# A state-space layer, linear attention and an FFN in one kernel: attention tokens transposed and stored by channel where their norm is made, and the FFN chains behind the main loop regrouped

## The chip, the cores and the metric

The kernel runs on one core of a Trainium2 chip. The metric is the device time of one execution in microseconds, as the median of three runs. The core has five engines with an instruction queue each, worked through in order: TensorE (PE in the profile; its weight loads are PEld), VectorE (DVE), ScalarE (ACT), GpSimd (POOL), and SyncE (SP), from which nearly all DMA transfers are issued. They meet only through semaphores.

## What is computed

The input x has 8 images of 96 channels and 64 x 64 pixels, so 4096 tokens of 96 channels each. Two layers follow each other:

```
x = x + mamba(group_norm(x))          # in_proj, conv of 4, silu, selective scan over 4096 tokens
                                      # with 192 channels x 16 states, gate, out_proj, LayerNorm
t = tokens(x)
t = t + attn(ln(t))                   # 6 heads, no softmax: y = q (k^T v) * 16**-0.5, then Wff
t = t + ffn(ln(t))                    # 96 -> 384 -> 96, operands rounded to fp8 e5m2, sums to fp16
x = from_tokens(t)
```

Since the attention has no softmax, all of it is one 96 x 96 matrix per image: from the Gram matrix of the normalised tokens (97 x 97 with a column of ones for the biases) come a few small products (W in the code), and then each token is multiplied by the result.

## The kernel before

**Tiling.** Images are taken in 4 pairs (p), tokens in 8 chunks of 512 (c), which makes 32 chunks (p, c). Partitions of the scan hold 32 channels x 4 states; a chunk is 24 units (u), each a scan over 2 x 512 elements for one block of 64 inner channels, 4 states and one image of the pair.

**The main loop** runs under manual scheduling: instructions go into each engine's queue in the order of the Python code. `unit()` writes one unit: the copy of the last state (L619), the matmul that spreads C over partitions (L571), the sums over states of an earlier unit (L595), the products dbu of three units ahead on GpSimd (L561), two scans on VectorE (L639), between them two exponentials on ScalarE for the next unit (L581, two PSUM buffers `da`), and the product with C (L663).

**Chains.** All other work is cut into generators, and the table `STEPS` says in which units each makes its next step, ahead of the scan or (after the bar) behind it:

- P prepares the chunk two ahead: norm, conv, projections, delta (L431 on). Its conv results leave PSUM on ScalarE (xm, L468), its delta by L511.
- E finishes the last chunk: out_proj (L691), LayerNorm, the residual in x1 (L741, L746), a second norm into `t1e` (tokens on partitions, 96 channels and a column of ones), the Gram matrix (L759, added up by L768), and the stores of x1 (L750) and `t1e` (L780) to DRAM.
- W turns the Gram matrix of a pair into the matrix of the attention (L793 to L816).
- F, one for each image of a chunk, nine chunks later (`LAG`), as the Gram matrix needs all chunks of a pair: it loads `t1e` as `tp` (L826) and x1 as x2 (L827), transposes `tp` by four matmuls with the identity (L831), copies the result to SBUF (`tT`, L834), multiplies by the attention's matrix (L838), adds (L844), norms (L398 to L411), transposes (L854, L857), and runs the FFN: three matmuls (L864) with copies (L871), ReLU (L877 or L881) and rounding to fp8 (L884), three matmuls back (L903), bias (L910 or L912), a transpose of x2 (L915), the sum and the store (L918, L919).

F0 is the F of image 1 of the pair and starts in unit 20, F1 that of image 0 and starts in unit 9. In the main loop E, F, W and the norms of the next pair (G) share two PSUM banks, mE and mF; F uses mE up to L838 and mF behind it.

**Behind the main loop** (from line 1012 on) the scheduler of the framework orders each engine's instructions, in the main by the order of the code. `run_out` steps its generators in turn; with `lag` a new one joins every `lag` turns. Four calls follow each other: the rest of the running chains with the last E; the two F of the last chunk of pair 2 (`tail_f(NP - 2)`); the two W of pair 3; and the 16 F of pair 3 with four PSUM banks and a lag of four. In these F, `tp` and x2 have four buffers; o2, qT, h8 and y16 have one each and h16 two.

Of the kernel before, what the change touches and what calls it, by code (L numbers as in the profile page):

```python
# [8 lines left out]
F32 = mybir.dt.float32  # L9
F32R = mybir.dt.float32r  # L10
F16 = mybir.dt.float16
F8 = mybir.dt.float8e5
# [3 lines left out]
C = 96  # L16
# [4 lines left out]
T = 512  # L21
NK = T // 128
# [6 lines left out]
AHEAD = 3  # L29
# [5 lines left out]


STEPS = {
    0: "F0 F1",
    1: "F0 F1 P",
    2: "F1 | F0 G0",  # L40
    3: "E P F1 | F0 G6",
    4: "E F1 | G6",
# [6 lines left out]
    11: "F0 E",  # L49
    12: "F0 E | P",  # L50
    13: "P E F0",
    14: "P F0 | E F1",
    15: "F1 E F0 P | G5",
    16: "| E F1 F0 W1 P",
    17: "P | F1 W1",
    18: "P P | W1 F1",
# [1 line left out]
    20: "E F0 P | W1 F1",  # L58
    21: "F1 P | E",
    22: "F1 P E",  # L60
    23: "F1 P | E F0",
}


# [1 line left out]
def tile_mamba_linear_attention_ffn(  # L66
# [29 lines left out]
    nc = tc.nc  # L96
    B, _, L = x.shape
    NP = B // 2
# [19 lines left out]
        return t  # L118

    def psum(tag="mp"):  # L120
        return ps_all.tile([128, T], F32, tag=tag, name=tag, bufs=2 if tag == "cc" else 1)


    ident = const.tile([128, 128], F32, name="ident")
# [266 lines left out]
    def norm_stats(src, n, tag):  # L391

        mv = p2.tile([128, n, 2], F32, tag=f"mv{tag}", name="mv")
        rstd = p2.tile([128, n], F32, tag=f"rs{tag}", name="rs")
        nmr = p2.tile([128, n], F32, tag=f"nm{tag}", name="nm")
        st = p2.tile([128, n, 6], F32, tag=f"st{tag}", name="st")
        for i in range(n):
            nc.vector.bn_stats(st[:, i, :], src[:, i, :])  # L398
        for i in range(n):
            nc.vector.bn_aggr(mv[:, i, :], st[:, i, :])  # L400

        def ends():
            nc.gpsimd.tensor_scalar_mul(nmr, mv[:, :, 0], -1.0)  # L403
            rsqrt(rstd, mv[:, :, 1], 1e-5)
            nc.gpsimd.tensor_mul(nmr, nmr, rstd)

        later("norms", ends)
        return rstd, nmr
# [266 lines left out]
    gram = {}  # L675
    kept = {}

    def chain_e(p, c, s):
        zs = s["zs"]
        o = t1e[:, :, 0:C]  # L680

        def half(t, b):
            return t[:, b * NK : (b + 1) * NK, :]

        def project(part):

            ps = psum("mE")
            for k in range(2):
                tok = (2 * part + k) * 128
                for j in range(NJ):  # L690
                    nc.tensor.matmul(  # L691
                        ps[:, 2 * k * C : 2 * (k + 1) * C], lhsT=zs[:, j, tok : tok + 128],
                        rhs=woT[:, j].rearrange("p b c -> p (b c)"),
                        start=(j == 0), stop=(j == NJ - 1),
                    )
            return ps

        def projected(part, ps):
            nc.scalar.copy(  # L699
                o.rearrange("p (b k) c -> p k b c", b=2)[:, 2 * part : 2 * part + 2],  # L700
                ps[:, 0 : NK * C].rearrange("p (k b c) -> p k b c", k=2, b=2),
            )

        def tokens(b):
            ps = psum("mE")
            for k in range(NK):
                nc.tensor.matmul(
                    ps[:, k * C : (k + 1) * C], lhsT=xr[:, b, k * 128 : (k + 1) * 128], rhs=idb,
                    start=True, stop=True,
                )  # L710
            return ps[:, 0 : NK * C].rearrange("p (k c) -> p k c", c=C)

        def scale(dst, src, norm, part):
            for i in range(2 * part, 2 * part + 2):
                normalise(dst[:, i, :], src[:, i, :], norm, i)

        def gains(b):
            nc.gpsimd.tensor_mul(
                half(o, b), half(o, b), gamma.unsqueeze(1).to_broadcast([128, NK, C])
            )  # L720

        nc.sync.dma_start(
            xr[0:C], x[2 * p : 2 * p + 2, :, c * T : (c + 1) * T].rearrange("b c t -> c b t")
        )
        ps = project(0)
        yield
        projected(0, ps)
        ps = project(1)
        yield
        projected(1, ps)  # L730
        yield
        norm = norm_stats(o, 2 * NK, "o")
        yield
        for part in range(4):
            scale(o, o, norm, part)
            yield
        gains(0)
        ps = tokens(0)
        yield
        x1 = p1.tile([128, 2 * NK, C], F32, tag="x1", name="x1")  # L740
        nc.vector.tensor_add(half(x1, 0), ps, half(o, 0))  # L741
        yield
        gains(1)
        ps = tokens(1)
        yield
        nc.vector.tensor_add(half(x1, 1), ps, half(o, 1))  # L746
        norm = norm_stats(x1, 2 * NK, "x")
        yield
        x1d = dram.tile([128, 2 * NK, C], F32, tag="x1d", name="x1d", bufs=NCH + 4)
        nc.sync.dma_start(x1d, x1)  # L750
        scale(o, x1, norm, 0)
        scale(o, x1, norm, 1)
        yield

        def products(b):
            ps = psum("mE")
            for k in range(NK):
                t = t1e[:, b * NK + k, :]
                nc.tensor.matmul(  # L759
                    ps[0 : C + 1, 0 : C + 1], lhsT=t, rhs=t, start=(k == 0), stop=(k == NK - 1)  # L760
                )
            return ps[0 : C + 1, 0 : C + 1]

        def collect(b, ps):
            if c == 0:
                nc.vector.tensor_copy(gram[p][:, b, :], ps)
            else:
                nc.vector.tensor_add(gram[p][:, b, :], ps, gram[p][:, b, :])  # L768

        if c == 0:  # L770
            gram[p] = p2.tile([C + 1, 2, C + 1], F32, tag="gram", name="gram")
        scale(o, x1, norm, 2)
        ps = products(0)
        yield
        collect(0, ps)
        scale(o, x1, norm, 3)
        yield
        ps = products(1)
        t1d = dram.tile([128, 2 * NK, C + 1], F32, tag="t1d", name="t1d", bufs=NCH + 4)
        nc.sync.dma_start(t1d, t1e)  # L780
        kept[p, c] = (x1d, t1d)
        yield
        collect(1, ps)


    attn_w = {}
# [29 lines left out]
        nc.vector.tensor_add(w[C : C + 1, b, :], ps[C : C + 1, 0:C], bffr[C : C + 1, :])  # L816


    def chain_f(p, c, b, banks, of_t1=None, of_x2=None):
        bank = banks[0]  # L820
        x1d, t1d = kept[p, c]
        blk = slice(b * NK, (b + 1) * NK)
        bufs = 4 if of_t1 else 1
        x2 = p2.tile([128, NK, C], F32, tag=of_x2 or f"x2{b}", name="x2", bufs=bufs)
        tp = p2.tile([128, NK, C + 1], F32, tag=of_t1 or "tp", name="tp", bufs=bufs)
        nc.sync.dma_start(tp, t1d[:, blk, :])  # L826
        nc.sync.dma_start(x2, x1d[:, blk, :])  # L827
        yield
        ps = psum(bank)
        for k in range(NK):  # L830
            nc.tensor.transpose(ps[0 : C + 1, k * 128 : (k + 1) * 128], tp[:, k, :], ident)  # L831
        yield
        tT = p2.tile([C + 1, T], F32, tag="rows", name="tT")
        nc.scalar.copy(tT, ps[0 : C + 1, :])  # L834
        yield
        ps = psum(bank)
        for k in range(NK):
# [7 lines left out]
        norm = norm_stats(x2, NK, f"f{b}")  # L845
        yield
        bank = banks[1]
        o2 = p1.tile([128, NK, C], F32, tag="o2", name="o2")
        for k in range(NK):
            normalise(o2[:, k, :], x2[:, k, :], norm, k)  # L850
        yield
# [1 line left out]
        for k in range(NK):  # L853
            nc.tensor.transpose(ps[0:C, k * 128 : (k + 1) * 128], o2[:, k, :], ident)  # L854
        yield
        qT = p1.tile([C, T], F8, tag="qT", name="qT")
        nc.scalar.activation(qT, ps[0:C, :], AF.Copy, saturate=False)  # L857
        yield
        h8 = []
# [7 lines left out]
            return ps  # L867

        def rounded(m, ps):
            h16.append(p2.tile([128, T], F16, tag="h16", name="h16"))  # L870
            nc.scalar.copy(h16[m], ps)  # L871

        def relu(m):
            if not m:
                h8.append(p1.tile([128, 3, T], F8, tag="h8", name="h8"))
            if of_t1:
                nc.vector.tensor_scalar(  # L877
                    h16[m], h16[m], b1q[:, m : m + 1], 0.0, ALU.add, ALU.max
                )
            else:  # L880
                nc.scalar.activation(h16[m], h16[m], AF.Relu, bias=b1q[:, m : m + 1])  # L881
            later(
                "others",
                lambda: nc.gpsimd.tensor_copy(h8[0][:, m, :], h16[m], saturate=False),  # L884
            )
# [18 lines left out]
                ps[0:C, :], lhsT=w2T[:, m, :], rhs=h8[0][:, m, :], start=(m == 0), stop=(m == 2)  # L904
            )
        yield
        y16 = p1.tile([C, T], F16, tag="y16", name="y16")
        nc.scalar.copy(y16, ps[0:C, :])
        if of_t1:
            nc.vector.tensor_scalar(y16, y16, b2q, None, ALU.add)  # L910
        else:
            nc.scalar.activation(y16, y16, AF.Identity, bias=b2q)  # L912
# [101 lines left out]
    gate(s, NJ - 1)  # L1014
    rest = [(p, c, b) for p in range(NP) for c in range(NCH) for b in range(2)]
    rest = rest[2 * (N - LAG) :]
    banks = ("mE", "mF", "cc", "y")

    def tail_f(p):
        return [  # L1020
            chain_f(*r, (banks[i % 4],) * 2, "dbu", "pr")
            for i, r in enumerate(r for r in rest if r[0] == p)
        ]

    run_out([*running.values(), chain_e(*chunks[N - 1], s)])
    run_out(tail_f(NP - 2), 4)
    run_out([chain_w(NP - 1, b, banks[b]) for b in range(2)])
    run_out(tail_f(NP - 1), 4)


# [51 lines left out]
```

## Time and profile before

| what | us |
|---|---|
| median of three runs (3532.91 to 3539.99) | 3535.59 |
| the profiled execution | 3550.77 |
| its span, first to last instruction | 3549.1 |
| VectorE busy | 3017.3 |
| TensorE busy, as modelled | 2708.4 |
| GpSimd busy | 2689.0 |
| ScalarE busy | 2277.4 |
| mean granted TensorE clock | 0.730 of full |

Times in the profile are counted from the start of the span. A row of the timeline has the start, the busy time, engine, line, operation, output and inputs, shapes, the number of instructions merged, and in brackets how long the engine was idle before and which instruction ended that. Matmul ends are modelled.

The chunks can be counted in the trace by their 48 scans. A chunk from the tenth on takes 98 to 109 us, one of the first nine, which have no F, 88 to 99 us. The last scan starts at 3366.2 us; what is behind it takes the remaining 183 us.

### The profile page before, as it was taken

What the parts mean: (1) busy time and instruction counts of PE and PEld (TensorE: products, weight loads), DVE (VectorE), ACT (ScalarE), POOL (GpSimd) and SP (SyncE); (2) the same over time, 40 slices, a digit from 0 to 9 for tenths busy, and PEclk for the clock granted to TensorE, in tenths of its full rate; (3) what the DMA queues carried; (4) which work ended last, traced back from release to release, by engine and by line L of the source; (5) the groups of instructions that cost most, each with busy time, mean ns of one, the idle gap of its engine ahead of it and who ended that gap; (6) DMA issues with size and microseconds to landing.
All of it is one profiled execution on the core that took longest, in us unless ns stands there. A gap on an engine that the chain in (4) does not pass through costs nothing.

```text
span 3549.1 us, 35756 instructions
## 1 busy us (share of the span) xinstructions
PE 2708.4 (76%) x9770; PEld 1011.7 (29%) x9770; DVE 3017.3 (85%) x4345; ACT 2277.4 (64%) x4347; POOL 2689.0 (76%) x1838
## 2 busy tenths in 40 slices
PE   5577777778787777877878877777788787887677
PEld 1122222222223222322223322222233232332244
DVE  2699999899998889888889888899888888988934
ACT  2456666566666666666666666666776766676556
POOL 1778888788878787778777778778877878777734
PEclk8667777677766787776787677778866777775667
DMA  2555555555554456554456554455544445545212
GB/s 80 127 128 139 134 141 142 143 131 133 136 149 107 104 139 154 138 129 108 112 139 154 131 138 105 117 134 150 149 124 121 99 121 144 152 119 139 72 59 61
DMA packets 252399, 444.05 MB, mean 125 GB/s; under 512 B 36965, under 2 KB 53542, under 8 KB 252198
## 3 DMA queue, kind: packets, MB, share of 16 engines
q1 hardware_dynamic: 248982, 441.70, 49.2%
q8 instruction: 77, 1.26, 0.2%
q14 instruction: 124, 1.02, 0.1%
q10 hardware_dynamic: 3216, 0.07, 0.1%
HBM read 349.24 MB, written 92.41 MB: 124 GB/s over the span
## 4 chain that ended last, share of the span: by engine, by line
DVE 39%; PE 25%; ACT 12%; issue 9%; POOL 7%; DMA 2%; SPq 1%; DVEq 0%; POOLq 0%; ACTq 0%
DVE hs L639 25%; PE mp L450 7%; DVE pr L663 7%; PE y L595 4%; POOL dbu L561 3%; DVE st L398 3%; ACT da L581 2%; PE cc L571 2%; PE mE L759 2%; PE mp L507 1%; PE mp L489 1%; PE mE L691 1%; POOL pr L670 1%; DVE mv L400 1%; DMA b<-bd 1%
## 5 line engine op out<-in xcount | busy, mean ns | idle before, releaser
L561 POOL TENSOR_TENSOR dbu<-du,b 128x1024 f32<-128x1024 f32 x768 | 1802.9, 2362 | 220.2 <-DVE hs L639 106.7
L639 DVE TENSOR_TENSOR_SCAN hs<-da,state,dbu 128x512 f32<-128x512 f32 x1290 | 1575.7, 1267 | 260.3 <-ACT da L581 252.2
L581 ACT ACTIVATE da<-dl,aneg 128x512 f32<-128x512 f32 x1474 | 999.1, 688 | 780.9 <-DVE hs L639 777.8
L663 DVE TENSOR_TENSOR pr<-hs,cc 128x1024 f32<-128x1024 f32 x640 | 777.6, 1215 | 36.8 <-DVE hs L639 0.5
L595 PE MATMUL y<-pr,ssum 128*32 128x512 f32 x3072 | 633.9, 883 | 4.9 <-DVE pr L663 4.9
L571 PE MATMUL cc<-cs,sel 64*128 64x512 f32 x640 | 397.2, 623 | 292.1 <-DVE pr L663 291.6
L450 PE MATMUL mp<-u,wk 96*64 96x512 f32 x1536 | 428.1, 683 | 90.3 <-ACT xm L468 86.9
L571 PEld LDWEIGHTS cc<-cs,sel 64*128 64x128 f32 x640 | 145.4, 229 | 932.3 <-DVE pr L663 423.0
L670 POOL TENSOR_TENSOR pr<-hs,c 128x1024 f32<-128x1024 f32 x128 | 301.7, 2357 | 122.6 <-DVE hs L639 96.4
L639 DVE TENSOR_TENSOR_SCAN hs<-da,dbu 128x512 f32<-128x512 f32 x184 | 213.5, 1207 | 110.9 <-ACT da L581 110.6
L884 POOL CAST h<-h 128x512 fp8e5<-128x512 f16 x192 | 117.5, 614 | 155.9 <-ACT h L881 109.9
L603 PE MATMUL y<-xm,dd 128*128 128x512 f32 x192 | 157.2, 913 | 99.5 <-DVE zs L609 99.3
L403 POOL TENSOR_SCALAR nm<-mv 128x8 f32<-128x8 f32 (+1 forms) x128 | 32.6, 255 | 238.8 <-DVE mv L400 222.0
L489 PE MATMUL mp<-xm,xpT 128*96 128x512 f32 x192 | 158.7, 994 | 48.7 <-ACT xm L483 48.0
L507 PE MATMUL mp<-dbl,dtT 12*128 12x512 f32 x192 | 168.0, 968 | 34.6 <-ACT cs L497 33.3
L864 PE MATMUL mF<-qT,w1T 96*128 96x512 fp8e5 x153 | 67.9, 444 | 157.1 <-ACT h L871 156.4
L450 PEld LDWEIGHTS mp<-u,wk 96*64 96x64 f32 x1536 | 105.0, 151 | 286.3 <-issue 162.9
L132 POOL TENSOR_TENSOR rs<-rs,mhalf 128x8 f32<-128x8 f32 (+1 forms) x128 | 173.5, 1355 | 10.7
L595 PEld LDWEIGHTS y<-pr,ssum 128*32 128x32 f32 x3072 | 75.2, 128 | 271.9 <-issue 228.1
L691 PE MATMUL mE<-woT,zs 128*128 128x192 f32 x768 | 142.9, 336 | 5.9 <-ACT t1e L699 4.3
L458 PE MATMUL mp<-u,wz 96*64 96x512 f32 x384 | 134.8, 788 | 14.6 <-ACT xm L476 11.7
L619 ACT COPY state<-hs 128x2 f32<-128x2 f32 x736 | 131.5, 179 | 0.2
(214 smaller groups left out, 3468.1 us busy)
## 6 DMA issues: line engine op xcount, KB each, us to landing
du<-lu SPq DMA_DIRECT2D x384, 256.0 KB, 5.2
dl<-ld SPq DMA_DIRECT2D x384, 256.0 KB, 7.2
b<-bd SPq DMA_DIRECT2D x512, 128.0 KB, 6.0
ld<-delta SPq DMA_DIRECT2D x96, 256.0 KB, 4.4
lu<-du SPq DMA_DIRECT2D x96, 256.0 KB, 4.9
c<-bd SPq DMA_DIRECT2D x128, 128.0 KB, 3.2
t1d<-t1e SPq DMA_DIRECT2D x32, 388.0 KB, 4.7
tp<-t1d SPq DMA_DIRECT2D x64, 194.0 KB, 5.9
```

Source lines behind the costliest of these rows:

```text
L132: nc.gpsimd.tensor_tensor(out_, out_, mhalf[0 : out_.shape[0], 0 : out_.shape[1]], op=ALU.pow)
L450: nc.tensor.matmul(ps[64 * b : 64 * b + 64, :], lhsT=wk[:, k, 64 * j : 64 * j + 64], rhs=u[:, b, k : k + T], start=(k == 0), stop=(k == 3),)
L489: nc.tensor.matmul(ps[0:C, :], lhsT=xpT[:, j, :], rhs=xm[:, j, :], start=(j == 0), stop=(j == NJ - 1),)
L507: nc.tensor.matmul(ps, lhsT=dtT[:, j, :], rhs=dbl[0 : 2 * RANK, :], start=True, stop=True)
L561: nc.gpsimd.tensor_mul(dbu, s["du", j][:, 2 * b : 2 * b + 2, :], s["b", g][:, b, :].unsqueeze(1).to_broadcast([128, 2, T]),)
L571: nc.tensor.matmul(cc, lhsT=sel[64:128, g, b], rhs=s["cs"][64:128, :], start=True, stop=True)
L581: nc.scalar.activation(da, s["dl", j][:, 2 * b + h, :], AF.Exp, scale=aneg[:, 2 * j + h, g : g + 1])
L595: nc.tensor.matmul(s["y"][q : q + 32, :], lhsT=ssum, rhs=pr[:, h, :], start=False, stop=(g == NG - 1),)
L639: nc.vector.tensor_tensor_scan(hs[:, h, :], s.pop(("da", u, h)), dbu[:, h, :], 0.0 if first else state["last"][:, u, h : h + 1], ALU.mult, ...
L663: nc.vector.tensor_mul(pr, hs, s.pop(("cc", u)).unsqueeze(1).to_broadcast([128, 2, T]))
L670: nc.gpsimd.tensor_mul(pr, s["hs", u], s["c", g][:, b, :].unsqueeze(1).to_broadcast([128, 2, T]))
L691: nc.tensor.matmul(ps[:, 2 * k * C : 2 * (k + 1) * C], lhsT=zs[:, j, tok : tok + 128], rhs=woT[:, j].rearrange("p b c -> p (b c)"), start= ...
```

## The change

1. **E transposes.** Behind the second Gram matrix, E transposes `t1e` image by image (four matmuls with the identity each), ScalarE copies the result to an SBUF tile `tT` [97, 512], and it is stored by channel. The store of `t1e` by token goes.
2. **F loads `tT` by channel** and multiplies at once. Its transposes and its ScalarE copy go, and two of its steps.
3. **STEPS** follow: E has two more steps, in units 0 and 1 of the next chunk; F0 loses the steps in units 23 and 0, F1 those in units 14 and 15.
4. **Behind the loop**: the running chains, the last E followed by the W of pair 3 (on banks `cc` and `mp`), and the two F of pair 2 (banks `y` and `da`) all run side by side; then the 16 F of pair 3 on six banks with a lag of three. Their tiles take buffers of the main loop: three for o2, two each for qT, h8 and y16, eight for x2, two h16 for even and two for odd chains.
5. The scratch `st` of the norms has one buffer in place of two.

```diff
@@ STEPS (lines that change)
-    0: "F0 F1",
-    1: "F0 F1 P",
+    0: "E F1",
+    1: "E F0 F1 P",
...
-    14: "P F0 | E F1",
-    15: "F1 E F0 P | G5",
+    14: "P F0 | E",
+    15: "E F0 P | G5",
...
-    23: "F1 P | E F0",
+    23: "F1 P | E",
@@ norm_stats
-        st = p2.tile([128, n, 6], F32, tag=f"st{tag}", name="st")
+        st = p1.tile([128, n, 6], F32, tag=f"st{tag}", name="st")
@@ chain_e(p, c, s, bank="mE"); every psum("mE") in it becomes psum(bank)
+        t1d = dram.tile([C + 1, 2, T], F32, tag="t1d", name="t1d", bufs=NCH + 4)
+
+        def transposed(b):
+            ps = psum(bank)
+            for k in range(NK):
+                nc.tensor.transpose(
+                    ps[0 : C + 1, k * 128 : (k + 1) * 128], t1e[:, b * NK + k, :], ident
+                )
+            return ps
+
+        def stored(b, ps):
+            tT = p2.tile([C + 1, T], F32, tag="rows", name="tT")
+            nc.scalar.copy(tT, ps[0 : C + 1, :])
+            nc.sync.dma_start(t1d[:, b, :], tT)
...
         ps = products(1)
-        t1d = dram.tile([128, 2 * NK, C + 1], F32, tag="t1d", name="t1d", bufs=NCH + 4)
-        nc.sync.dma_start(t1d, t1e)
+        yield
+        collect(1, ps)
+        ps = transposed(0)
+        yield
+        stored(0, ps)
+        ps = transposed(1)
+        yield
+        stored(1, ps)
         kept[p, c] = (x1d, t1d)
-        yield
-        collect(1, ps)
@@ chain_f(p, c, b, banks, lane=None)
-        tp = p2.tile([128, NK, C + 1], F32, tag=of_t1 or "tp", name="tp", bufs=bufs)
-        nc.sync.dma_start(tp, t1d[:, blk, :])
+        x2 = p2.tile(
+            [128, NK, C], F32, name="x2", **place(f"x2{b}", ("pr", "b")[(lane or 0) % 2], 4)
+        )
+        tT = p2.tile([C + 1, T], F32, name="tT", **place("tp", "dbu", AHEAD + 1))
+        nc.sync.dma_start(tT, t1d[:, b, :])
         nc.sync.dma_start(x2, x1d[:, blk, :])
-        yield
-        ps = psum(bank)
-        for k in range(NK):
-            nc.tensor.transpose(ps[0 : C + 1, k * 128 : (k + 1) * 128], tp[:, k, :], ident)
-        yield
-        tT = p2.tile([C + 1, T], F32, tag="rows", name="tT")
-        nc.scalar.copy(tT, ps[0 : C + 1, :])
         yield
...
-        o2 = p1.tile([128, NK, C], F32, tag="o2", name="o2")
+        o2 = p2.tile([128, NK, C], F32, name="o2", **place("o2", "hs", 3))
...
-        qT = p1.tile([C, T], F8, tag="qT", name="qT")
+        qT = p2.tile([C, T], F8, name="qT", **place("qT", "zs", 2))
...
+            to = dict(tag=("du", "dl")[lane % 2] if after else "h16")
+            h16.append(p2.tile([128, T], F16, name="h16", **to))
...
+                h8.append(p2.tile([128, 3, T], F8, name="h8", **place("h8", "xm", 2)))
...
+        y16 = p2.tile([C, T], F16, name="y16", **place("y16", "pq", 2))
@@ behind the main loop
-    run_out([*running.values(), chain_e(*chunks[N - 1], s)])
-    run_out(tail_f(NP - 2), 4)
-    run_out([chain_w(NP - 1, b, banks[b]) for b in range(2)])
-    run_out(tail_f(NP - 1), 4)
+    def ends(before):
+        yield from before
+        yield from chain_e(*chunks[N - 1], s, "cc")
+        yield
+        ws = [chain_w(NP - 1, b, ("cc", "mp")[b]) for b in range(2)]
+        while ws:
+            ws = [w for w in ws if next(w, "end") != "end"]
+            yield
...
+    run_out(
+        [
+            ends(running.pop("E")), running.pop("F1"), behind(running.pop("F0"), 3),
+            *running.values(), *tail_f(NP - 2, ("y", "da")),
+        ]
+    )
+    run_out(tail_f(NP - 1, ("mE", "mF", "cc", "y", "mp", "da")), 3)
```

## The prediction

> **What bounds the kernel now.** First the page's groups: they say what the scan, VectorE's main work, waits for.
>
> ```profile
> L639 DVE TENSOR_TENSOR_SCAN hs<-da,state,dbu 128x512 f32<-128x512 f32 x1290 | 1575.7, 1267 | 260.3 <-ACT da L581 252.2
> L639 DVE TENSOR_TENSOR_SCAN hs<-da,dbu 128x512 f32<-128x512 f32 x184 | 213.5, 1207 | 110.9 <-ACT da L581 110.6
> ```
>
> VectorE is busy for 85% of the span and waits for little but ScalarE's exponentials: 252 + 111 = 363 us. In the main loop (3255 us) only what moves these waits counts. Read between the scans chunk by chunk, they lie in three places: some 6 us before the scan of unit 12 (ScalarE has SiLU and two table loads there; untouched), 2 to 4 us before that of unit 16, and 1 to 3 us before that of unit 4. Second, the timeline of one chunk around unit 16:
>
> ```profile
> 1969.54 2.07 PE L507 MATMUL mp<-dbl,dtT 12*128 12x512 f32 x2
> ...
> 1971.55 1.51 PE L903 MATMUL mF<-h,w2T 128*96 128x512 fp8e5 x3
> ...
> 1972.85 1.06 PE L831 MATMUL mE<-ident,tp 128*97 128x128 f32 x4
> ...
> 1973.95 0.59 ACT L834 COPY tT<-mE 97x512 f32<-97x512 f32 x1 [4.92 <-PE mE L831]
> 1974.43 0.58 ACT L908 CAST y<-mF 96x512 f16<-96x512 f32 x1
> ...
> 1975.05 0.72 ACT L912 ACTIVATE y<-y,b2q 96x512 f16<-96x512 f16 x1
> 1975.68 0.67 ACT L511 ACTIVATE delta<-mp,dtb 128x512 f32<-128x512 f32 x1
> ...
> 1976.25 1.29 ACT L581 ACTIVATE da<-dl,aneg 128x512 f32<-128x512 f32 x2
> ...
> 1977.03 2.46 DVE L639 TENSOR_TENSOR_SCAN hs<-da,state,dbu 128x512 f32<-128x512 f32 x2 [3.56 <-ACT da L581]
> ```
>
> ScalarE stands 4.92 us for F1's transposes, at the end of a line on TensorE, and everything behind goes late into the scan. Third, the timeline of the next chunk from unit 1 to 4:
>
> ```profile
> 2017.89 0.69 ACT L468 ACTIVATE xm<-mp,cb 128x512 f32<-128x512 f32 x1
> 2018.46 1.31 ACT L581 ACTIVATE da<-dl,aneg 128x512 f32<-128x512 f32 x2
> ...
> 2018.63 3.12 PE L450 MATMUL mp<-u,wk 96*64 96x512 f32 x8 [2.17 <-ACT xm L468]
> ...
> 2031.11 0.58 ACT L908 CAST y<-mF 96x512 f16<-96x512 f32 x1 [1.72 <-PE mF L903]
> ...
> 2033.13 1.28 DVE L639 TENSOR_TENSOR_SCAN hs<-da,state,dbu 128x512 f32<-128x512 f32 x1 [2.79 <-ACT da L581]
> ```
>
> From 2018.63 TensorE runs without a gap through L450, L603, L595, L571, L691, L450 and L903, to the copy that ScalarE waits for. What delays L468 delays the scan of unit 4. Last, the stages behind the loop:
>
> ```profile
> 3367.00:3400.00 33.00, 21.41 (x100) 14.66 (x97) 10.52 (x50) 17.51 (x38) 11.35 (x19) 0.71 0.17 52
> 3400.00:3428.00 28.00, 19.68 (x78) 11.48 (x77) 9.83 (x38) 9.62 (x20) 7.13 (x14) 0.62 0.24 74
> 3428.00:3545.00 117.00, 95.26 (x408) 59.89 (x406) 56.29 (x226) 74.97 (x160) 57.12 (x112) 0.76 0.22 63
> ```
>
> The columns are stage, its length, PE, PEld, DVE, ACT and POOL busy, the granted clock, the DMA share and GB/s. No engine is full. In the first row the last E runs (its last Gram sum, L768, ends at 3400.9); in the second two lone F, then W (its last, L816, ends at 3428.3); in the third 16 F. There L844 of bank mE comes at 3453.2, 3480.6 and 3508.3: four banks turn over in 27.6 us, 6.9 us a chain, by the length of a chain and not by an engine.
>
> **Part by part: the main loop.**
>
> *Unit 16 (gain).* F1's four L831 and its L834 leave units 14 and 15. ScalarE's next work there, L908, needs only L903, which ends at 1973.06; it now starts at 1974.43, so about 1.3 us go (1.28 here; 1.33 in the next chunk). What is late next is L903 itself; 2.2 us of the 3.56 stay. The wait is over 2 us in 19 of the 23 chunks with an F1: 19 x 1.3 = -25 us. Bounds: 0, if GpSimd or the gate is late at once; -37, if half as much again closes up.
>
> *Units 23 to 2 (loss).* F0's L831 in unit 23 and L834 in unit 0 are replaced by E's own: same shapes (0.6 to 1.1 and 0.59 us), same places, nothing. E's second image adds four transposes to TensorE's queue in unit 0 and a copy ahead of ScalarE's in unit 1; behind that wait the FFN's copy, L468 and the two exponentials. The exponential of unit 2 has room: it ends at 2019.15 and its scan starts at 2020.36, 1.2 us against about 0.5 (what 0.59 adds when pipelined, as 1973.95 to 1974.43). L468 has none: TensorE's gapless line starts 0.5 us later, and up to 0.9 at the lower clock, as F0's L838 now has to wait for the bank mE until that copy is done. I take 0.6 in the 19 chunks where unit 4 waits about 1 us or more: +11. Bounds 0 and 19 x 1.2 = +23. The first nine chunks have no F behind the loss, and their unit 4 waits 0.1 us: nothing.
>
> *SP and DMA.* The store of `t1e` (388 KB, 4.7 us to landing) becomes two of 194 KB, one issue (0.33 us) more. They stand behind the eight loads of du and dl in unit 0 and hold up the load of xr, issued at 1910.3 in the chunk of the first timeline and needed by L707 at 1965.0. A `tT` is read nine chunks later, and F1 loads it 7 units ahead of its use, as `tp` was 5. Nothing. If that cover went, each transfer would be worth its 5 to 6 us. The bytes per F are the same. Here the Trainium skill speaks against the change: "SBUF — State Buffer", section "Door 1: The DMA port swizzle", gives a transfer that leaves out partitions fewer ports; 97 rows of 2048 bytes put 16 KB instead of 12 KB on the fullest port, by its 27.2 GB/s an estimated 0.15 us a transfer. No row here shows that, and hidden it adds nothing to the sum.
>
> The scratch `st` is written and read by VectorE alone: nothing. Sum of the loop: -25 + 11 = -14 us.
>
> **Behind the loop.** *From E's end to W's end.* Now 3400.9 to 3428.3, 27.4 us. In the new order two transposes with copies (3400.95 to 3402.58 for one such pair, 1.6 us) and W are left. A round of W (matmul, VectorE copy) takes 0.98 us alone (L801 at 3420.60, L808 at 3421.58); four rounds with two images in turn I take at 1.3 each, with 0.5 us for the last copies 5.7. So 7.3 in place of 27.4: -20. E itself: its second projection no longer waits for mE (copies L699 at 3373.47 and 3379.75; some 3.7 us won), but the two F now beside it put 2 x 4.1 us on ScalarE, partly ahead of E's scalings, and a norm's wait for GpSimd blocks ScalarE's queue. I take E to end 2 us later: -18. Bounds: -24 (3.7 won, 8.2 hidden in ScalarE's 15.5 idle us) and -8 (8.2 exposed and W at 4 x 2 us, the pace of 3419.3 to 3428.3).
>
> *The 16 F.* From W to the last store's issue it is 117.4 us (3428.3 to 3545.7), 20 to the first store and 6.5 us for each of 15 more. Per chain TensorE has 95.26 / 16 = 5.95 us; without four L831 (12.56 us for 56 records of them in this stage, 0.90 a chain) 5.05. ScalarE has 74.97 / 16 = 4.69, without L834's 0.58 4.11. Six banks over a chain some 2 us shorter would give 25.6 / 6 = 4.3 us, so TensorE becomes the bound: 5.05 at best. Nobody here fills TensorE; I take 92%, 5.5 us, and 18 us to the first store: 18 + 15 x 5.5 = 100.5, or -17. Bounds: -24 (5.05) and -2 (6.5).
>
> The clock decides between these: granted 0.62 in the second row and 0.76 in the third, L838 takes 0.275 us at the full and 0.421 at the half clock. By "TensorE: Matmul & The Clock Gate", section "Part 1: The HAM clock gate (the "warmup" mystery)", the full clock comes after a busy window of about 3.4 us and goes after an idle one, so six chains should keep it; the third row agrees in part, as it flips all the same at 81% busy. By the rule alone the period would go below 5.
>
> **Sum.** -14 - 18 - 17 = -49 us. The profiled execution has 3550.8 (span 3549.1 and 1.7 around it): 3501.8. It lies 15.2 us above the median of the runs, so the median becomes 3486.6: **3487 us**.
>
> **Rivals.**
> - *The last stage stays where it is* (chance 0.15). With six chains TensorE, at half clock, sets 6.3 us: -5 in place of -17; 3499. For it: the clock flips now. Against: 20% of TensorE idle.
> - *Unit 4 takes back what unit 16 gave* (0.15): +23 against -25; 3499. For it: the gapless line.
> - *More closes up* (0.14): period 5.05, W at -22, unit 16 at full price with unit 4 hidden: -25 - 22 - 24 = -71; 3465.
> - *The stand moves to unit 1* (0.1, the other side). ScalarE stands at E's second copy as it now does at F1's, because TensorE in unit 0 has the conv, L595 and the FFN's matmul ahead of the transposes. It decides once they end over 1.2 us behind the state's copy; now L595 ends 1.6 us ahead of that copy's end at the full clock (1909.3 and 1910.9) and 0.4 ahead at the half (3276.5 and 3276.9), with 0.7 or 1.1 us of transposes to follow. At a price of 2.5 us, a little under unit 16's, in 31 chunks it is +78, with the -49: 3565.
> - That the change doesn't do what it says is out: the program has the new order.
>
> **How the numbers follow.** The forecast has 0.46. The range 3455 to 3517 holds it, the two rivals at 3499 and most of the one at 3465; it leaves out the last rival and the corners where all bounds fall on one side (-85: 3451; +13: 3549). A measurement tells 0.2% (7 us) from no change; faster than 3528.5 are the first four cases, less 0.03 for that upper corner: 0.87; within 0.02; slower 0.11, the last rival and the corner.
>
> **What would show it.** Right: the wait before unit 16's scan near 2.2 us with L908 behind L903, that before unit 4's up by 0.5; W's end some 9 us behind E's; stores 5.5 us apart, TensorE over 90% busy. Wrong: ScalarE idle at E's copy in unit 1; stores over 6 us apart.

## The result, and the profile after

| kernel | time (median) | ratio to before, 95% interval | span of its profiled execution |
|---|---|---|---|
| before, measured beside it | 3537.79 us | | 3549.1 us |
| the changed kernel | 3666.35 us | 1.036 (1.035 to 1.038) | 3666.0 us |

The forecast was 3487 us; the change made the kernel 129 us slower. The last scan starts at 3442.1 us where it started at 3366.2, so 76 us came in the main loop, and the time behind it grew from 183 to 224 us, 41 more.

The page's groups after, first the two of the scan. The second had 110.9 us of waits before and is unchanged; the first had 260.3. The third is F's multiplication by the attention matrix, which takes `tT`:

```profile
L639 DVE TENSOR_TENSOR_SCAN hs<-da,state,dbu 128x512 f32<-128x512 f32 x1290 | 1574.7, 1265 | 304.1 <-ACT da L581 295.1
...
L639 DVE TENSOR_TENSOR_SCAN hs<-da,dbu 128x512 f32<-128x512 f32 x184 | 213.4, 1205 | 110.6 <-ACT da L581 110.4
...
L858 PE MATMUL mE<-attw,tT 97*128 97x96 f32 x392 | 84.1, 383 | 107.1 <-DMA tT<-t1d 91.6
```

Read the last columns of the third row: TensorE stood 107 us before it, 91.6 of them for a transfer, the load of `tT`; the waits place all of these in the loop, 18 of them, and each is in F0, which loads `tT` in unit 20 and multiplies in unit 1 of the next chunk. F1, which loads in unit 9 and multiplies in unit 16, waits for none. Before, the first reader of the load (then `tp`) was L831, and it waited 4.1 us in all. The timeline of after, from the issue of that load to the scan that came late (TensorE's weight loads and other work left out):

```profile
2031.95 0.23 SPq L853 DMA_DIRECT2D tT<-t1d  x1
...
2037.95 9.23 SPq L536 DMA_DIRECT2D du<-lu  x4
...
2043.70 0.70 ACT L468 ACTIVATE xm<-mp,cb 128x512 f32<-128x512 f32 x1
...
2046.50 2.00 PE L858 MATMUL mE<-attw,tT 97*128 97x96 f32 x8 [5.06 <-DMA tT<-t1d]
...
2048.42 3.68 PE L450 MATMUL mp<-u,wk 96*64 96x512 f32 x8
...
2059.51 0.85 PE L924 MATMUL mF<-h,w2T 128*96 128x512 fp8e5 x3
...
2060.39 0.58 ACT L929 CAST y<-mF 96x512 f16<-96x512 f32 x1 [2.16 <-PE mF L924]
...
2062.41 2.46 DVE L639 TENSOR_TENSOR_SCAN hs<-da,state,dbu 128x512 f32<-128x512 f32 x2 [5.59 <-ACT da L581]
```

F0's load was issued in unit 20, five units ahead of its reader, and the reader could start only 14.5 us after that issue. The bank `mp`, which L450 writes, was free at 2044.4 (end of L468), but L450 stands behind L858 in TensorE's queue; the gapless line of the prediction starts 4 us late and the scan waits 5.59 us. (The prediction calls this the wait before the scan of unit 4. Counted from the chunk's first scan it lies between unit 4's scans and unit 5's; the name is kept.) Why the load takes so long stands in the DMA view of after for 2028 to 2048, 40 slices of 0.5 us, busy share in tenths and GB/s:

```profile
DMA  9999999999999999888869959997110000000074
GB/s 262 217 303 397 410 410 408 430 352 368 400 267 246 172 266 295 164 220 210 177 183 291 205 143 356 213 176 123 33 49 20 29 25 25 25 28 26 25 90 111
```

From 2042 to 2046.5 the DMA engines are all but idle, and what moves is some 25 GB/s: in the trace 12 packets of 2048 bytes a microsecond, each of some 84 ns, one after another. That is one engine of the 16, working off the rest of `tT`'s 97 rows; 97 times 80 ns is 7.8 us. It began while that engine, like all, was full of other transfers. In the same way, behind the loop (3475 to 3485, slices of 0.25 us), a store of `tT`, which SP issued at 3474.3 and which has the same 97 rows, runs alone from 3475.75 until it ends at 3482.3:

```profile
GB/s 147 332 234 31 25 33 25 25 25 25 25 25 25 33 25 25 25 25 25 25 25 33 25 25 25 25 25 25 25 27 25 68 154 356 246 43 25 25 25 33
```

Before, the same bytes went as `tp`, 128 rows of 1552 bytes, in slices of up to 317 GB/s, and landed 2.7 us after their issue there. The stages behind the loop, in the columns of the prediction (last E; W; 16 F):

```profile
3442.00:3504.50 62.50, 36.06 (x154) 25.27 (x154) 18.96 (x80) 26.66 (x58) 19.09 (x34) 0.64 0.17 58
3504.50:3509.30 4.80, 3.58 (x23) 2.78 (x21) 2.29 (x10) 0.59 (x1) 0.00 (x0) 0.86 0.18 52
3509.30:3665.00 155.70, 84.84 (x350) 55.38 (x349) 57.46 (x224) 65.37 (x144) 57.10 (x112) 0.65 0.15 48
```

W now ends 4.8 us behind E, as the new order promised; but E takes 62.5 us in place of 34.7 and the 16 F 155.7 in place of 117, with every engine less busy than before.

### The profile page after: what moved, and what is told of

It reads as the page before. It is cut to its first block, busy times and chain, and to the rows that moved or that the text cites. A ratio compares the mean times of both kernels' runs of the same rounds, so it can differ in the third digit from the quotient of the medians.

```text
span 3666.0 us, 35738 instructions
## 1 busy us (share of the span) xinstructions
PE 2732.9 (75%) x9770; PEld 1030.5 (28%) x9770; DVE 3018.1 (82%) x4345; ACT 2275.5 (62%) x4347; POOL 2689.6 (73%) x1838
## 5 line engine op out<-in xcount | busy, mean ns | idle before, releaser
L450 PE MATMUL mp<-u,wk 96*64 96x512 f32 x1536 | 438.8, 698 | 44.9 <-ACT xm L468 41.5
L603 PE MATMUL y<-xm,dd 128*128 128x512 f32 x192 | 167.3, 968 | 82.2 <-DVE zs L609 82.1
L450 PEld LDWEIGHTS mp<-u,wk 96*64 96x64 f32 x1536 | 107.4, 156 | 240.9 <-issue 171.8
L858 PE MATMUL mE<-attw,tT 97*128 97x96 f32 x392 | 84.1, 383 | 107.1 <-DMA tT<-t1d 91.6
L691 PE MATMUL mE<-woT,zs 128*128 128x192 f32 x744 | 139.3, 338 | 0.2
```

The source lines that it names most:

```text
L450: nc.tensor.matmul(ps[64 * b : 64 * b + 64, :], lhsT=wk[:, k, 64 * j : 64 * j + 64], rhs=u[:, b, k : k + T], start=(k == 0), stop=(k == 3),)
L603: nc.tensor.matmul(s["y"], lhsT=dd[:, j, :], rhs=s["xm"][:, j, :], start=True, stop=False)
```

## The experiments

Two theories. **A**: all of it is the shape of the transfers of `tT`. **B**: E's steps in units 0 and 1 and the six chains cost it, whatever the transfers look like.

**e1_split.** Same bytes, same order, each transfer cut where the ones row begins:

```
-            nc.sync.dma_start(t1d[:, b, :], tT)
+            nc.sync.dma_start(t1d[0:C, b, :], tT[0:C])
+            nc.sync.dma_start(t1d[C : C + 1, b, :], tT[C : C + 1])
...
-        nc.sync.dma_start(tT, t1d[:, b, :])
+        nc.sync.dma_start(tT[0:C], t1d[0:C, b, :])
+        nc.sync.dma_start(tT[C : C + 1], t1d[C : C + 1, b, :])
```

> The changed kernel with each 97-row transfer of tT (store and load) cut in two, 96 rows and 1 row; nothing else is altered. In the trace of the changed kernel a 97-row transfer moved as 97 packets of 2048 B one after another, 25 GB/s, about 7.7 us, and L858 stood 5.06 us for one in the loop. Theory A (the shape of the transfers costs all of it): the 96-row parts land in under 3 us behind the loop and L858 waits for no load; time near the forecast, 3487 us, ratio to before 0.98 to 0.995; the wait before unit 4 back to 2 to 3 us, stores 5.5 us apart. Theory B (E's steps in units 0 and 1 and six chains side by side cost it, whatever the transfers look like): within 20 us of the changed kernel, ratio 1.03 to 1.04, and the wait before unit 4 stays near 6 us with TensorE or ScalarE as its releaser.

Measured 3491.33 us, ratio 0.985 (0.981 to 0.988): 175 us less than the changed kernel, and 4 us from the forecast. F's multiplication, now L860, waits for no load anywhere. Theory B falls. Its page's groups of the scan and its stages behind the loop (E; W; 16 F):

```profile
L639 DVE TENSOR_TENSOR_SCAN hs<-da,state,dbu 128x512 f32<-128x512 f32 x1290 | 1574.7, 1265 | 251.8 <-ACT da L581 248.6
...
L639 DVE TENSOR_TENSOR_SCAN hs<-da,dbu 128x512 f32<-128x512 f32 x184 | 213.3, 1205 | 103.8 <-POOL dbu L561 72.2
```

```profile
3350.00:3389.50 39.50, 30.93 (x154) 20.40 (x150) 18.83 (x80) 26.19 (x58) 18.67 (x34) 0.78 0.26 81
3389.50:3394.00 4.50, 3.17 (x22) 2.34 (x22) 2.33 (x11) 0.59 (x1) 0.00 (x0) 1.00 0.42 132
3394.00:3491.00 97.00, 74.77 (x349) 48.72 (x348) 55.83 (x224) 65.05 (x144) 57.63 (x112) 0.77 0.25 74
```

The waits that ScalarE's exponentials end fall from 295 to 249 us in the first group, and the stages shrink from 62.5, 4.8 and 155.7 us to 39.5, 4.5 and 97.0. The last scan starts at 3350.0.

**e2_split_old_end.** e1_split with the lines behind the loop as they were before (four banks, `chain_w` between the two groups of F); the E of the chunk before the last is finished ahead of the last E.

> e1_split with the stages behind the loop in the order of before (F and the last E in turn, four banks, W behind two F), so that against before only the loop is changed, and against e1_split only what is behind it. Theory A: loop -14 us as forecast and four L831/L834 a chain fewer behind it: 3510 to 3525 us, ratio 0.993 to 0.997, some 25 to 35 us over e1_split. Theory B: loop about 70 us longer than before, ratio 1.015 to 1.025.

Measured 3510.39 us, ratio 0.990 (0.987 to 0.994). The last scan starts at 3349.4, and behind it lie 163.2 us, against 182.9 in before (so F without its four transposes and a copy, and with the added buffers of its tiles, which stay in this run, is worth some 20) and 141.8 in e1_split (so the new order, six banks and a lag of three are worth 21).

**e1s_split_store and e1l_split_load**: half of e1_split's edit each.

> Only the stores of tT are cut into 96 rows and 1 row; the loads keep their 97 rows. e4_before_store97, with 97-row stores that nobody reads, was no longer than before up to the last scan and some 70 us longer behind it. Theory A1 (it is the loads that cost, for L858 waits for their landing and SP's later issues stand behind them): 3600 to 3650 us, ratio 1.015 to 1.03, unit 4's wait still near 6 us. Theory A2 (it is the stores, which fill the one engine that the loads then need): 3500 to 3530 us, unit 4's wait near 3 us.

> Only the loads of tT are cut into 96 rows and 1 row; the stores keep their 97 rows. Theory A1 (the loads cost): within 15 us of e1_split, 3490 to 3505 us, unit 4's wait near 3 us, the stages behind the loop some 142 us as there. Theory A2 (the stores cost): 3590 us or more.

Measured 3648.94 us, ratio 1.032 (1.028 to 1.035), with the stores alone cut, and 3505.13 us, 0.991 (0.988 to 0.994), with the loads alone cut. It is the loads (A1). With 97-row loads alone (e1s_split_store) the last scan starts at 3438.9, 89 us behind e1_split's, and the mean wait of unit 4 over 20 chunks with an F is 6.42 us (6.17 in the changed kernel, 2.89 in e1_split); its row of F's matmul, here L859, shows the same wait:

```profile
L859 PE MATMUL mE<-attw,tT 97*128 97x96 f32 x392 | 87.6, 395 | 116.1 <-DMA tT<-t1d 88.7
```

With 97-row stores alone (e1l_split_load) the loop is e1_split's (the last scan starts at 3350.0) and 152 us lie behind it in place of 142. The last E issues its two stores at 3390.6 and 3392.9; between the loads that follow, the DMA engines move 25 GB/s until 3410.5, and the matmul of the fifth of the 16 F, on bank `mp`, stands 7.5 us (to 3409.8) for a load that was issued behind those stores. That F reads a chunk that was stored long before, so it doesn't wait for the data of these stores; that its load stands behind them on the one engine fits the view and was not tried.

**e4_before_store97 and e5_before_store96.** The disputed transfer without the change: a useless store in before's `chain_f`, of 97 rows in e4 and of 96 in e5.

```
         nc.scalar.copy(tT, ps[0 : C + 1, :])
+        scr = dram.tile([C + 1, T], F32, tag="scr", name="scr", bufs=4)
+        nc.sync.dma_start(scr[0 : C + 1], tT[0 : C + 1])
```

> The kernel before with one useless store of each F's tT, all 97 rows, to a scratch that nothing reads: the order of all other work is that of before. Theory A (a 97-row transfer is one engine's work of about 7.7 us, in which later transfers queue behind it): 56 or more of them in the loop and 16 behind it cost tens of us, +20 to +100, ratio 1.006 to 1.03, and the trace shows 97 packets of 2048 B at about 25 GB/s. Theory B (the transfers are covered): +0 to +5 us.

> As e4_before_store97, but rows 0 to 95 alone are stored (1% fewer bytes). Theory A: the bytes spread over many engines at over 100 GB/s and cost next to nothing, 0 to +10 us. Theory B: the same as e4_before_store97 within 3 us. If both cost alike and much, it is the issue on SP or the later release of tT, and not the shape.

Measured 3610.68 us, ratio 1.018 (1.014 to 1.023), and 3548.33 us, 1.002 (0.999 to 1.004): one row less, and 62 us less. The DMA views for 3441 to 3461, e4 first, then e5:

```profile
GB/s 220 171 25 29 25 25 25 29 25 25 25 29 25 25 25 25 29 25 25 57 29 25 25 25 29 25 25 41 29 25 25 25 25 29 25 25 25 29 25 46
```

```profile
GB/s 0 0 0 0 0 37 175 370 197 8 0 22 149 227 92 244 410 213 209 56 205 205 230 225 227 68 0 0 53 258 307 168 0 0 0 0 0 0 0 22
```

In e4 one engine works for 19 us without a break (25 GB/s), and ScalarE's next copy into that buffer waits 48.1 us in all for such stores behind the loop. In its loop, where nothing waits for them, they cost nothing (the last scan starts at 3354.7).

**e11_rows.** Is it 97, or being over 96? The same useless store with another number of rows for each image of a chunk:

```
+        n = (97, 96, 95, 94, 93, 92, 91, 89)[(2 * c + b) % 8]
+        scr = dram.tile([n, T], F32, tag=f"scr{n}", name=f"scr{n}", bufs=4)
+        nc.sync.dma_start(scr, tT[0:n])
```

> The kernel before with one useless store of each F's tT, of 97, 96, 95, 94, 93, 92, 91 or 89 rows in turn, each 2048 B, to see what the duration follows. The Trainium skill's "DMA: Bandwidth & Descriptors", section "Why a DMA increments its semaphore by 16 and not by 1", has the number of engines as the largest divisor, up to 16, of the rows: 1, 16, 5, 2, 3, 4, 13 and 1. At the 79 ns a packet of the changed kernel's trace the shortest of each would last about 7.7, 0.5, 1.5, 3.7, 2.4, 1.8, 0.6 and 7.0 us, and some 2 us to landing on top. Rival: a last row beyond 96 is what is slow; then 97 alone lasts 7.7 us and all others about as 96.

Its one execution took 3574.79 us. In the loop other transfers hide the streams, so the figures are those behind it. The DMA views of 10 us from just before two of the last issues, slices of 0.25 us, first of 89 rows, then of 91; with each goes a result of 192 KB:

```profile
GB/s 0 0 0 16 16 156 188 139 90 74 57 57 74 41 25 25 25 25 25 25 25 25 33 25 25 25 25 25 25 25 33 25 25 25 25 25 25 25 0 0
```

```profile
GB/s 0 0 0 123 213 254 336 336 197 66 41 0 0 0 0 0 0 0 0 0 0 0 0 0 0 0 0 0 0 0 0 16 8 90 156 229 66 82 82 41
```

89 rows, a prime number under 96, draw a tail of 25 GB/s until 9.4 us; 91 are done, result and all, by 2.7 us. Of 94 the tail ran at two packets at a time and ended about 6 us after the issue. So it is not the row beyond 96. The Trainium skill has it in "DMA: Bandwidth & Descriptors", section "Why a DMA increments its semaphore by 16 and not by 1": a transfer is given the largest number of engines, up to 16, that divides the slowest dimension of both sides. All that could be told apart here (97, 94, 91 and 89 rows) agrees; 95, 93 and 92 could not be separated from the result beside them.

**e10_loads_from_act.** Is it slow because it stands in SP's queue? The changed kernel with `nc.scalar.dma_start(tT, t1d[:, b, :])`.

> The changed kernel, 97 rows a transfer, with the loads of tT alone issued from ScalarE's queue. Theory E (the load is slow as one engine moves its 97 packets, wherever it is issued): L858 waits for it as before, 3630 to 3680 us, and ScalarE's issues may be held up as SP's were. Theory S (it is slow as it stands behind SP's other transfers and holds up SP's next issues): unit 4's wait falls to about 3 us and the time behind the loop below 190 us, 3510 to 3580.

Measured 3723.29 us, ratio 1.052 (1.047 to 1.057), the slowest of all and 43 us above the range of theory E too. Theory S falls: unit 4's mean wait is still 5.1 us, and now ScalarE's queue is held at its issues, up to 15 us for one (the third number; SP's longest was 9.8 us):

```profile
L853 ACTq DMA_DIRECT2D tT<-t1d x64: 216/217/15017, 982.4 to 3672.3; - x64
```

**e6_p_first, e7_f1_first, e9_p_and_f1_first and e8_before_p_first.** What is left in e1_split is unit 4's wait, which the prediction did expect to grow. Two orders attack it, on top of e1_split; e9 has both, and e8 has the first on before.

The first, P ahead in unit 1 (in e8 from "F0 F1 P" to "P F0 F1"):

```
-    1: "E F0 F1 P",
+    1: "P E F0 F1",
```

The second, F1 ahead in units 3 and 4:

```
-    3: "E P F1 | F0 G6",
-    4: "E F1 | G6",
+    3: "F1 E P | F0 G6",
+    4: "F1 E | G6",
```

> e1_split with P ahead of E and F0 in unit 1, so that L468 is ahead of E's second copy in ScalarE's queue and TensorE's line from L450 starts earlier. In e1_split that line runs from L450 at 2005.64 to L926, which ends at 2017.95, and the wait before unit 4's scan is 2.89 us as a mean, 0.93 over before's. If E's copy ahead of L468 is what made unit 4 worse: 0.5 to 0.9 us less in some 20 chunks, -10 to -18 us against e1_split, 3473 to 3482. If the rest of the line sets it (L603, which waits for VectorE, or the clock): within 5 us of e1_split.

> e1_split with F1 ahead of E (and P) in units 3 and 4, so that L926 is ahead of L691 and the second L450 on TensorE, and the copy L931 ahead of L699 on ScalarE. L691 and L450 took 4.1 us between L571 and L926 in e1_split. If the end of TensorE's line is what unit 4's scan waits for: L931 comes some 4 us earlier, the exponential then waits for L699 behind L691, and 1.3 to 2.5 of the 2.9 us go in 20 chunks, -25 to -50 us against e1_split, 3441 to 3466. If GpSimd's products or E's norm are late next: within 10 us of e1_split.

> The kernel before with one thing altered, P ahead of F0 and F1 in unit 1, as in e6_p_first (which was 48 us faster than e1_split, its wait before unit 4's scan 0.98 us in place of 2.89). It tells whether that order is a gain of its own or mends what the change broke. In before the wait of unit 4 is 1.96 us. If a gain of its own: unit 4 falls to about 1 us, -15 to -25 us, 3515 to 3525. If it only mends E's copy ahead of L468, which before doesn't have: within 7 us of before.

> e1_split with both orders, P first in unit 1 (e6_p_first, 3443) and F1 first in units 3 and 4 (e7_f1_first, 3442). If both shorten the same line of TensorE to L926, the second adds little, as another releaser of unit 4's scan is late next (0.98 us stays in both): 3430 to 3443. If they add: -96 us against e1_split, 3395.

| kernel | time | ratio to before (95%) | unit 4's mean wait | clock granted from unit 1's scan to unit 4's, mean |
|---|---|---|---|---|
| before | 3535 to 3543 us | 1 | 1.96 us | 0.77 |
| e1_split | 3491.33 | 0.985 (0.981 to 0.988) | 2.89 | 0.70 |
| e6_p_first | 3443.47 | 0.973 (0.970 to 0.976) | 0.98 | 1.00 |
| e7_f1_first | 3442.26 | 0.973 (0.970 to 0.976) | 0.98 | 0.72 |
| e9_p_and_f1_first | 3448.12 | 0.973 (0.970 to 0.977) | 0.99 | 1.00 |
| e8_before_p_first | 3545.14 | 1.002 (0.999 to 1.004) | 2.08 | 0.79 |

e6's -48 us is far beyond the 10 to 18 expected, and the last column points to why. Timelines, first e1_split, then e6_p_first, of TensorE around the chunk's first L450:

```profile
2003.96 1.13 PE L860 MATMUL mE<-attw,tT 97*128 97x96 f32 x8 [1.33 <-ACT tT L782]
2005.64 3.68 PE L450 MATMUL mp<-u,wk 96*64 96x512 f32 x8 [0.55 <-ACT xm L468]
```

```profile
1981.20 1.94 PE L450 MATMUL mp<-u,wk 96*64 96x512 f32 x8 [1.43 <-ACT xm L468]
1983.07 1.13 PE L860 MATMUL mE<-attw,tT 97*128 97x96 f32 x8
```

In e1_split TensorE stands twice, 1.33 us for E's second copy to free the bank mE and 0.55 us for L468; at the second the granted clock falls from 1.00 to 0.50, and L450 takes 3.68 us. The same two stands lie in all 21 chunks, and in 20 of them the clock falls. In e6 it stands once, 1.43 us, and the clock stays at full up to unit 4's scan in each of the 21 chunks with an F. The Trainium skill, in "TensorE: Matmul & The Clock Gate", section "Part 1: The HAM clock gate (the "warmup" mystery)", has the clock fall after an idle window of some 3.4 us; the 1.88 us in two pieces here were enough.

That the clock makes most of the wait can be read within single programs, where the order of the work and the stand before this L450 are the same in every chunk and the clock falls in some of them. In e8 TensorE stands 1.93 or 1.94 us before this L450 in all 21 chunks: where the clock stays at full (8 chunks) the wait of unit 4 is 0.94 us as a mean, where it falls (13) it is 2.83. In before, with a stand of 2.15 to 2.17 us, it is 1.07 (3 chunks) and 2.08 (18); in e1_split 1.07 (1) and 2.99 (20). In e8 nothing is won in sum: P first is no gain of its own.

e7 leaves the clock low and takes L691 and a L450 out of the way of L926. Together they add nothing (e9 lies 5 us above the range expected of it): in all three what is left is some 1.0 us, and in e6 ScalarE is then busy without a gap from its scaling for the norm (L411) through both copies to the exponential.

## Why the prediction was wrong, step by step

- **SP and DMA: "Nothing. If that cover went, each transfer would be worth its 5 to 6 us."** This is the step that failed, alone, and two things in it were wrong. The durations taken were those of 128-row transfers, for a transfer of 97 rows; the trace of before has none. A load on one engine takes 7.8 us at least, 14.5 in the loop shown above, beside other transfers. And the cover was judged by F1 alone, whose lead of 7 units does suffice: its matmul comes 33 to 46 us behind the issue of its load and never waits. F0's lead is 5 units, and there the reader starts 14 to 20 us behind the issue, after waits of mostly 4 to 6 us. The price of this step: 89 us in the loop and 63 behind it for the loads alone (e1s_split_store), with the stores 92 and 82. The rule weighed there, on ports, gave an estimated 0.15 us; that was the wrong rule, since not the port but the number of engines decided.
- **"The bytes per F are the same"** is true, and told nothing.

With that term put right (e1_split), the rest can be checked. The sum came out, 3491 us for 3487, but partly by luck. The profiles of before and e1_split differ by 57 us and not by the 49 forecast; that of before lay 15.2 us above its median, as the prediction allowed for, that of e1_split only 2.4 above its own, so a miss of 8 us and one of 13 the other way leave 4. The terms, from these two profiles:

| term | forecast | e1_split against before |
|---|---|---|
| unit 16's wait | -25 | 2.99 to 1.59 us as a mean of 20 chunks: -28 |
| unit 4's wait | +11, bound +23 | 1.96 to 2.89 us: +19 |
| whole loop | -14 | 3366.2 to 3350.0: -16 |
| E's end against the last scan | +2 | 34.7 to 39.5: +5 |
| E's end to W's end | 27.4 to 7.3 | 27.4 to 4.5 |
| both of these | -18 | -18 |
| 16 F, W's end to the last store's issue | 117.4 to 100.5 | 117.4 to 95.0 |

- *The whole loop*: the terms of units 16 and 4 explain 9 of the 16 us. The rest is open and may be no more than the spread of executions: with before's order of work, the last scan starts at 3366.2 us in before, 3354.7 in e4, 3362.7 in e5 and 3364.3 in e11.
- *Unit 16* went as described. In e1_split the copy, here L931, stands behind L926 and nothing else, and some 2.06 us are left:

```profile
1959.89 1.51 PE L926 MATMUL mF<-h,w2T 128*96 128x512 fp8e5 x3
...
1961.44 0.58 ACT L931 CAST y<-mF 96x512 f16<-96x512 f32 x1 [3.90 <-PE mF L926]
...
1964.03 2.46 DVE L639 TENSOR_TENSOR_SCAN hs<-da,state,dbu 128x512 f32<-128x512 f32 x2 [2.06 <-ACT da L581]
```

- *Unit 4*: L468 starts 0.48 us later after unit 1's scan (1.60 to 2.08; 0.5 was taken). What was mis-sized is the wait for the bank mE and the clock that it costs: 0.6 was taken where 0.93 came, within its bound.
- *The last stage*: the first store is issued 20.5 us after W's end (18 taken), and the others follow at 4.97 us (5.5 taken, 5.05 called the best). The reason given was wrong: TensorE is busy for 77% of the stage, not over 90%, and needs 4.67 us a chain, not 5.05. Which engine or wait sets the 4.97 us was not tried.
- *The rival on the slower side* put a stand in unit 1 too, but ScalarE's, for E's transposes. In the changed kernel it is TensorE that stands there, for the load. The place was right and the mechanism was not.

The experiments also give what beats both kernels: split transfers with one of the two orders, 3442 to 3443 us, 2.7% under before.

## What to carry to other kernels

When a change moves the same bytes in another shape, look at the number of rows first: cut a 97-row transfer into 96 and 1, or choose rows that 16 divides, don't take its duration from a row of another shape, and hold it against the lead of every reader, not of one. A DMA view that shows long runs at 25 GB/s is one engine at work; look for who waits at its end. When an edit puts a second stand into TensorE's line, look at the granted clock behind it before counting the stand alone.

## What the runs showed that was not expected

- A transfer on one engine holds up its queue's later issues as well. The four issues of `du` above stretch over 9.23 us, 7.0 of them between the second and the third, where the next four, of `dl`, took 1.80. By the waits of SP's queue the third stood until the load of `tT` landed: SP's transfers take eight semaphores in turn, and it needed the one of that load. Up to the last scan SP stood 150.2 us for this, in 22 waits (e1_split: 7.3 us in 19). Single issues also last long themselves, those of a `tT` load up to 9.8 us on SP and 15.0 on ScalarE; why was not tried.
- The 97-row stores cost nothing in the loop and some 11 us behind it, the loads of the same rows 89 and 63: what counts is who waits, not the transfer.
- Two stands of 1.33 and 0.55 us within 3.1 us halved TensorE's clock in 20 of 21 chunks, and one of 1.43 us in none. In before and in e8, with one stand of 2.16 and 1.94 us in every chunk, the clock stayed at full in 3 and in 8 of 21 chunks. So the length of a stand alone doesn't decide in between; what does was not tried.
